# Attention over a 64 x 64 image: the order of the products that accumulate the upper and the middle part of the output

## The chip, the cores and the metric

The kernel runs on one core of one Trainium2 chip. The metric is the device time of one execution in microseconds, from the first to the last instruction of the core. Every number of the trace is from one profiled execution on that core.

## The reference, cut to what matters

The input `x` has shape (4, 64, 64, 256): four images, each with N = 4096 positions and C = 256 channels, all float32. Three projections feed one attention step, and the result is added to the input:

```python
q = einsum('bwhc,cd->bwhd', x, Wq) + bq      # d = 128
k = einsum('bwhc,cd->bwhd', x, Wk) + bk      # d = 128
v = einsum('bwhc,cd->bwhd', x, Wv) + bv      # d = 256
pq, pk, pv = (t.reshape(B, -1, N) for t in (q, k, v))
energy = einsum('bcn,bcm->bnm', pq, pk)      # 4096 x 4096 for each image
attention = softmax(energy, axis=-1)
out = einsum('bcm,bnm->bcn', pv, attention)
return gamma * out.reshape(B, W, H, C) + x
```

For each image there are two large products: the energies (4096 x 4096 with a contraction over 128) and the output (256 x 4096 with a contraction over 4096 keys).

## The kernel before, in words

**Arithmetic.** The large products run in the type that the profile calls fp32r[...]. To get the accuracy back, every operand is split. A softmax weight `x` becomes an upper part `h` (line 349, ScalarE), a rest `l` (line 355, VectorE) and a correction `d` (line 358, VectorE); the values are split in the same way into `vh`, `vl` and `vd`. The output is `h·vh + l·vl + d·vd`, up to scales. `vh` and `vl` carry two columns of ones behind their 256 channels, so that the sum of the weights (the denominator of the softmax) comes out of the same products: these products have 258 columns. The products with `vd` have 256.

**Tiling.** An image's 4096 rows are cut into `NG` = 16 groups of 256, and every group into `NJ` = 2 halves `j` of 128. The keys are cut into 32 tiles of 128, named `m`, and four of them make a unit: `NU` = 8 units `t` in a group, `STEPS` = 128 units in an image, 512 in the whole kernel.

**One unit on TensorE** is 36 products (a weight load and a matmul each), in this order:

1. `energy` (line 317, matmul at line 330): twelve products for the unit three further on. They go to two PSUM tiles, `sa` (two products into each half of it) and `sb` (one), in the sequence sa, sa, sb.
2. `attend` (line 363, matmul at line 383), three families of eight: `h` with `vh`, `l` with `vl`, `d` with `vd`. In each family the half `j` is the outer loop and the key tile `i` (0 to 3) the inner one. The product (j, i) has `left[:, i, j*128:(j+1)*128]` as its weights and row `m = 2t + i//2 + 16*(i%2)` of `vh`, `vl` or `vd` as its moving operand. The families h and l both accumulate into `acc[j]`, which is one PSUM bank for each half (tiles `a0` and `a1`, called `a` in the profile); the family d accumulates into the tile `bb`, one bank for both halves.

In one place the loop before has another order: for the family l, half j = 1, in the units t = 1 and t = 3 of every group, the four key tiles are taken backwards (`back`, line 379).

**Around it.** ScalarE turns the energies into two exponentials (line 334) and makes `h`; VectorE multiplies the exponentials (line 344) and makes `l` and `d`. The whole part runs under a manual schedule: the order of the instructions on each engine is that of the code, and the loop at lines 509 to 551 sets it. `h` is made two units ahead of its use, `l` and `d` one unit ahead. `h` has three buffers, `l` and `d` two each. The keys of a unit come by DMA from a copy in DRAM (line 314), into one of three buffers.

**End of a group.** After the eighth unit ScalarE copies `acc[0]` and `acc[1]` out of PSUM (line 394). `finish` (line 396) then scales, transposes (line 415) and writes the group, spread over the next units. The next group writes its first h products into the same two banks, after the eight products of d and the twelve energies that lie between. The last group of all goes through `finish_last` (line 427).

**Accumulation flags.** A matmul with `start` begins an accumulation in its bank. Before the change each of `a0` and `a1` gets it on product i = 0 of its half in the family h of unit t = 0, and `bb` on the first product of d.

At the start of each image there are projections (lines 122, 135, 156), which the change does not touch.

Of the kernel before, what the change touches and what calls it, by code (L numbers as in the profile page):

```python
# [2 lines left out]

# [17 lines left out]
def kernel(  # L21
# [36 lines left out]
    nc = tc.nc  # L58
    B, W, H, C = x.shape
    P = 128  # L60
# [4 lines left out]
    NI = NM // 2  # L65
# [108 lines left out]
    NJ = NB // P  # L174
    NG = N // NB
    NU = NM // 4
# [22 lines left out]
    with ExitStack() as fast:  # L199
# [18 lines left out]
        vh = qkv.tile([P, NM, VC], F32R, tag="vh", name="vh")  # L218
        vl = qkv.tile([P, NM, VC], F32R, tag="vl", name="vl")
        vd = qkv.tile([P, NM, C], F32R, tag="vd", name="vd")  # L220
# [131 lines left out]
        def halves(b, u):  # L352
# [7 lines left out]
            )  # L360
            units[b, u] = h, l, d

        def attend(b, u):

            g, t = divmod(u, NU)
            if t == 0:
                now["acc"] = [
                    ps_o.tile([P, C + 2], F32, tag=f"a{j}", name=f"a{j}_{b}_{g}")
                    for j in range(NJ)
                ]  # L370
                now["bb"] = ps_o.tile([P, NJ, C], F32, tag="bb", name=f"bb_{b}_{g}")
            h, l, d = units[b, u]
            acc, bb = now["acc"], now["bb"]
            for left, right in ((h, vh), (l, vl), (d, vd)):
                for j in range(NJ):
                    out_ = bb[:, j, :] if left is d else acc[j]


                    back = left is l and j == NJ - 1 and t in (1, 3)
                    for i in reversed(range(4)) if back else range(4):  # L380
                        m = 2 * t + i // 2 + NI * (i % 2)

                        nc.tensor.matmul(  # L383
                            out_,
                            left[:, i, j * P : (j + 1) * P],
                            right[:, m, : out_.shape[1]],
                            start=(t == i == 0 and (left is h or left is d and j == 0)),
                            stop=(t == NU - 1 and i == 3 and left is not h),
                            skip_group_check=True,
                        )  # L390
            if t == NU - 1 and (b, g) != (B - 1, NG - 1):
                o = now["o"] = work.tile([P, NJ, C + 2], F32, tag="o", name=f"o_{b}_{g}")
                for j in range(NJ):
                    nc.scalar.activation(o[:, j, :], acc[j], AF.Identity, scale=1.0 + E)
# [89 lines left out]
        for b in range(B):  # L484
# [24 lines left out]
            for u in range(STEPS):  # L509
                g, t = divmod(u, NU)  # L510
# [33 lines left out]
                for forms in beside:  # L544
                    next(forms)
                attend(b, u)
                if (b, u) == (B - 1, STEPS - 1):
                    finish_last(b, g, loads.pop((b, "x", g)))
# [10 lines left out]
    NG = N // NB  # L559
    NJ = NB // P  # L560
    NP = NM // 2
    xg, og = columns(x, NB), columns(out, NB)
    with tc.If(nc.values_load(again[0:1, 0:1]) > 0), ExitStack() as general:
# [8 lines left out]
        for b in range(B):  # L572
# [16 lines left out]
            for g in range(NG):  # L589
                ps = []  # L590
                mx = work.tile([P, 2, NB], F32, tag="mx", name=f"gmx_{b}_{g}")
                for t in range(NP):
                    sp = ps_s.tile([P, 2, NB], F32, tag="s", name=f"gs_{b}_{g}_{t}")
                    for h in range(2):
# [4 lines left out]
                            start=True,  # L599
                            stop=True,  # L600
# [31 lines left out]
                for t, p in enumerate(ps):  # L632
# [8 lines left out]
                    for h in range(2):  # L641
                        for s in range(2):
# [4 lines left out]
                                start=(t == h == 0),  # L647
                                stop=(2 * t + h == NM - 1),
# [6 lines left out]
                r = work.tile([P, NB], F32, tag="r", name=f"gr_{b}_{g}")  # L655
# [36 lines left out]
```

## Time and profile before

The time is 2447.39 us, the median of two runs (2447.21 to 2447.56). The profiled execution has a span of 2445.0 us at a granted TensorE clock of 0.999.

| engine | busy us | share of the span | instructions |
|---|---|---|---|
| TensorE, matmuls | 2434.4 | 100% | 19988 |
| TensorE, weight loads | 2403.8 | 98% | 19988 |
| VectorE | 2100.4 | 86% | 2318 |
| ScalarE | 1797.5 | 74% | 3201 |
| GpSimd | 425.8 | 17% | 781 |

| products | line | number | mean duration of one, ns | columns |
|---|---|---|---|---|
| energy into sa | 330 | 4096 | 279 | 256 |
| energy into sb | 330 | 2048 | 276 | 256 |
| h with vh, into a | 383 | 4096 | 282 | 258 |
| l with vl, into a | 383 | 4096 | 282 | 258 |
| d with vd, into bb | 383 | 4096 | 278 | 256 |

How to read it: matmuls are pipelined, so the duration of one (some 280 ns) is not what one costs. What one costs is the distance from its start to the start of the next, which is what the chain of waits adds up. A unit takes about 4.2 us.

### The profile page before, as it was taken

To read this page: it belongs to the slowest core of one execution; us is meant where nothing else is said; L and a number is where in the kernel's file an instruction comes from. 1 tells how busy PE (TensorE), PEld (TensorE's weight loads), DVE (VectorE), ACT (ScalarE), POOL (GpSimd) and SP (SyncE) were. 2 spreads that over 40 slices of the span, in tenths; PEclk is the share of its full clock that TensorE was granted. 3 is DMA by queue.
4 is the path that set the end of the run, shared out by engine and by line. 5 is a ranking of instruction groups with operands and counts; after the bars stand their busy time and mean duration, and the time that the engine had idled before them with its cause. 6 is when DMAs were issued, how large, how long until landed. Compare 5 with 4: busy or idle time off the path is not lost.

```text
span 2445.0 us, 50042 instructions
## 1 busy us (share of the span) xinstructions
PE 2434.4 (100%) x19988; PEld 2403.8 (98%) x19988; DVE 2100.4 (86%) x2318; ACT 1797.5 (74%) x3201; POOL 425.8 (17%) x781
## 2 busy tenths in 40 slices
PE   9999999999999999999999999999999999999998
PEld 8999999999899999999989999999998999999998
DVE  5988888888698888888869888888886988888887
ACT  5777777777677777777667777777766777777775
POOL 4211111111411111111141111111114111111110
PEclk9999999999999999999999999999999999999999
DMA  7766666665776666666477666666647766666663
GB/s 233 225 201 213 203 207 202 203 214 156 232 225 197 210 204 207 209 197 212 145 241 229 202 201 207 205 209 201 205 143 245 230 204 198 210 204 209 207 202 114
DMA packets 137407, 498.92 MB, mean 204 GB/s; under 512 B 15536, under 2 KB 57264, under 8 KB 137168
## 3 DMA queue, kind: packets, MB, share of 16 engines
q0 software_dynamic: 92320, 453.17, 59.8%
q1 hardware_dynamic: 44304, 42.22, 5.5%
q8 instruction: 160, 2.62, 0.4%
q14 instruction: 79, 0.65, 0.1%
q10 hardware_dynamic: 544, 0.26, 0.0%
HBM read 445.25 MB, written 50.33 MB: 203 GB/s over the span
## 4 chain that ended last, share of the span: by engine, by line
PE 99%; DMA 0%; DVE 0%; SPq 0%; issue 0%
PE a L383 40%; PE bb L383 19%; PE sa L330 19%; PE sb L330 10%; PE qk L135 5%; PE v L156 5%; PE xt L122 1%; PE ot L415 1%; DMA x<-in_x_dram 0%; SPq L82 0%; DVE o L452 0%; PE ot L457 0%; DVE x L463 0%; PE zp L449 0%; DVE r L441 0%
## 5 line engine op out<-in xcount | busy, mean ns | idle before, releaser
L334 ACT ACTIVATE x<-sa 128x512 f32<-128x512 f32 x1024 | 614.2, 600 | 507.6 <-PE sa L330 505.4
L344 DVE TENSOR_TENSOR x<-x,y 128x1024 f32<-128x1024 f32 x512 | 627.0, 1225 | 228.2 <-ACT y L334 228.2
L330 PE MATMUL sa<-q,k 128*128 128x256 f32 x4096 | 733.2, 279 | 0.0
L355 DVE TENSOR_TENSOR l<-x,h 128x1024 fp32r<-128x1024 f32 x512 | 624.0, 1219 | 0.0
L358 DVE SCALAR_TENSOR_TENSOR d<-h,x 128x1024 fp32r<-128x1024 f32 x512 | 624.0, 1219 | 0.0
L330 PEld LDWEIGHTS sa<-q,k 128*128 128x128 f32 x4096 | 617.9, 188 | 0.4
L334 ACT ACTIVATE y<-sb 128x512 f32<-128x512 f32 x1024 | 615.1, 601 | 0.0
L383 PE MATMUL a<-vh,h 128*128 128x258 f32 x4096 | 574.3, 282 | 0.0
L383 PE MATMUL a<-vl,l 128*128 128x258 f32 x4096 | 571.9, 282 | 0.0
L330 PE MATMUL sb<-q,k 128*128 128x256 f32 x2048 | 566.2, 276 | 0.0
L383 PE MATMUL bb<-vd,d 128*128 128x256 f32 x4096 | 556.3, 278 | 0.0
L314 POOL DMA_DIRECT2D k<-kf x512 | 279.8, 546 | 1566.6 <-PE sb L330 1541.7
L349 ACT ACTIVATE h<-x 128x1024 fp32r<-128x1024 f32 x512 | 543.9, 1062 | 9.1 <-DVE x L344 8.4
L383 PEld LDWEIGHTS a<-vl,l 128*128 128x128 f32 x4096 | 524.6, 189 | 0.0
L383 PEld LDWEIGHTS a<-vh,h 128*128 128x128 f32 x4096 | 522.7, 189 | 0.0
L383 PEld LDWEIGHTS bb<-vd,d 128*128 128x128 f32 x4096 | 513.7, 188 | 0.0
L330 PEld LDWEIGHTS sb<-q,k 128*128 128x128 f32 x2048 | 384.9, 188 | 0.1
L135 PE MATMUL qk<-wqk_sb,xts 128*128 128x256 f32 x512 | 121.1, 379 | 0.0
L156 PE MATMUL v<-xts,wv_sb 128*128 128x256 f32 x512 | 120.3, 379 | 0.0
L156 PEld LDWEIGHTS v<-xts,wv_sb 128*128 128x128 f32 x512 | 97.3, 190 | 13.2
L135 PEld LDWEIGHTS qk<-wqk_sb,xts 128*128 128x128 f32 x512 | 92.3, 190 | 10.0
L275 POOL DMA_DIRECT2D qd<-qks x128 | 69.4, 550 | 179.5 <-DVE qks L144 170.3
(60 smaller groups left out, 868.6 us busy)
## 6 DMA issues: line engine op xcount, KB each, us to landing
k<-kf POOLq DMA_DIRECT2D x512, 768.0 KB, 4.7
x<-in_x_dram SPq DMA_DIRECT2D x128, 256.0 KB, 3.9
kf<-f POOLq DMA_DIRECT2D x64, 384.0 KB, 3.7
out_dram<-x POOLq DMA_DIRECT2D x63, 256.0 KB, 2.5
qd<-qks POOLq DMA_DIRECT2D x128, 64.0 KB, 2.9
qr<-qd SPq DMA_DIRECT2D x64, 128.0 KB, 3.6
wv_sb<-in_L_conv_Wv_dram POOLq DMA_DIRECT2D x1, 256.0 KB, 6.3
out_dram<-x SPq DMA_DIRECT2D x1, 256.0 KB, 3.5
```

Source lines behind the costliest of these rows:

```text
L122: nc.tensor.transpose(tp[:, k, s, :], self.xs[i][:, s, k * P : (k + 1) * P], ident,)
L135: nc.tensor.matmul(qk[:, s, :], self.xt[i][:, k, s, :], wqk_sb[:, k, :], start=(k == 0), stop=(k == KC - 1),)
L156: nc.tensor.matmul(vp[:, eh, :], wv_sb[:, k, eh * P : (eh + 1) * P], self.xt[i][:, k].rearrange("p s a -> p (s a)"), start=(k == 0), stop= ...
L275: nc.gpsimd.dma_start(qd[b, i // 2 + NG // 2 * s][:, i % 2, :], x[:, s, :C2])
L314: nc.gpsimd.dma_start(t.rearrange("p (i s) f d -> p i s (f d)", s=2), kf[b, u % NU])
L330: nc.tensor.matmul(to[:, i], kt[:, 2 * k + i, f, :], q[:, f], start=first, stop=last)
L334: nc.scalar.activation(to[:, 2 * k : 2 * k + 2, :], sp.rearrange("p i j d -> p i (j d)"), AF.Exp, scale=scale,)
L344: nc.vector.tensor_tensor(x, x, y, ALU.mult)
L349: nc.scalar.activation(h, units[b, u], AF.Identity, scale=UPPER)
L355: nc.vector.tensor_tensor(l, x, h.bitcast(F32), ALU.subtract)
L358: nc.vector.scalar_tensor_tensor(d, h.bitcast(F32), 1.0 + E, x, ALU.mult, ALU.subtract)
L383: nc.tensor.matmul(out_, left[:, i, j * P : (j + 1) * P], right[:, m, : out_.shape[1]], start=(t == i == 0 and (left is h or left is d and ...
```

## The change

The eight products of the family h, and the eight of the family l, no longer run j outside and i inside. For each unit a sequence of the eight pairs (j, i) is drawn at random, with a fixed seed, when the program is built. The draw has two stages. First it is drawn which four of the eight places go to the key tiles i = 0, 1 (with m even) and which to i = 2, 3 (with m odd); of the 70 ways to choose four of eight, 64 different ones are used for each family and each t, one for each of the 64 groups of the kernel. Then the order within each half is shuffled. The family d keeps its order. The backward order of units 1 and 3 goes away with the loop that held it.

So the change makes the sequence of weights, moving operands and target banks vary from unit to unit, where before it repeated. The products themselves, their number, their operands and the buffers are the same. `start` now goes to the first product that is issued into a bank, whichever that is, and `stop` to the last two places of a family in the last unit.

```diff
+        chance = Random(5)
+        halves_of_8 = list(combinations(range(8), 4))
+        orders = [[chance.sample(halves_of_8, B * NG) for _ in range(NU)] for _ in range(2)]
+
+        def order(f, b, g, t):
+            if f == 2:
+                return [(j, i) for j in range(NJ) for i in range(4)]
+            low, high = ([(j, i) for i in r for j in range(NJ)] for r in ((0, 1), (2, 3)))
+            chance.shuffle(low)
+            chance.shuffle(high)
+            first = orders[f][t][b * NG + g]
+            return [(low if x in first else high).pop() for x in range(8)]
...
-            for left, right in ((h, vh), (l, vl), (d, vd)):
-                for j in range(NJ):
+            begun = set()
+            for f, (left, right) in enumerate(((h, vh), (l, vl), (d, vd))):
+                for n, (j, i) in enumerate(order(f, b, g, t)):
                     out_ = bb[:, j, :] if left is d else acc[j]
-                    back = left is l and j == NJ - 1 and t in (1, 3)
-                    for i in reversed(range(4)) if back else range(4):
-                        m = 2 * t + i // 2 + NI * (i % 2)
-                        nc.tensor.matmul(
-                            out_,
-                            left[:, i, j * P : (j + 1) * P],
-                            right[:, m, : out_.shape[1]],
-                            start=(t == i == 0 and (left is h or left is d and j == 0)),
-                            stop=(t == NU - 1 and i == 3 and left is not h),
-                            skip_group_check=True,
-                        )
+                    bank = 2 if left is d else j
+                    m = 2 * t + i // 2 + NI * (i % 2)
+                    nc.tensor.matmul(
+                        out_,
+                        left[:, i, j * P : (j + 1) * P],
+                        right[:, m, : out_.shape[1]],
+                        start=(t == 0 and bank not in begun),
+                        stop=(t == NU - 1 and n >= 6 and left is not h),
+                        skip_group_check=True,
+                    )
+                    begun.add(bank)
```

More of the change, by code (lines that the diff above doesn't have):

```diff
@@ L1 @@
 from contextlib import ExitStack
-from itertools import cycle
+from itertools import combinations, cycle
+from random import Random
 import concourse.bass as bass
```

## The prediction, written before the result was known

> **What bounds the kernel now.** I read the page first. Its chain of work that ended last says who sets the end:
>
> ```profile
> PE 99%; DMA 0%; DVE 0%; SPq 0%; issue 0%
> PE a L383 40%; PE bb L383 19%; PE sa L330 19%; PE sb L330 10%; PE qk L135 5%; PE v L156 5%; PE xt L122 1%; PE ot L415 1%; DMA x<-in_x_dram 0%; SPq L82 0%; DVE o L452 0%; PE ot L457 0%; DVE x L463 0%; PE zp L449 0%; DVE r L441 0%
> ```
>
> TensorE is the chain. The products that the change reorders, `a` at line 383, are 40% of it, the largest single piece. Next, the view of waits, for TensorE alone:
>
> ```profile
> PE xt L122 <- DMA x<-in_x_dram: 1.2, 1, 1.2
> PE wp L197 <- DVE ones L88: 1.1, 1, 1.1
> PE zp L449 <- DVE zs L447: 0.5, 1, 0.5
> PE ot L457 <- DVE o L452: 0.2, 1, 0.2
> ```
>
> That is all: 3.0 us of waiting in 2445, none of it before a product of line 383. So no order of products can win time by waiting less, and the question is only whether a product costs more or less in another place, or whether a new wait arises. What a product costs is read from the chain in order of time, for one unit:
>
> ```profile
> 1003.87 0.23 PE sa L330 x2
> 1004.10 0.11 PE sb L330
> 1004.21 0.23 PE sa L330 x2
> 1004.44 0.11 PE sb L330
> 1004.55 0.23 PE sa L330 x2
> 1004.78 0.11 PE sb L330
> 1004.89 0.23 PE sa L330 x2
> 1005.12 0.11 PE sb L330
> 1005.23 1.91 PE a L383 x16
> 1007.14 0.93 PE bb L383 x8
> ```
>
> Columns are start, length, product and count. Twelve energies take 1005.23 - 1003.87 = 1.36 us, 113.3 ns each; sixteen a products 1.91 us, 119.4 ns each; eight bb products 0.93 us, 116 ns each. The a products are thus some 5 ns dearer than their two extra columns explain (258/256 x 113.3 = 114.2). That excess, 5.2 ns x 8192 = 43 us, is all that an order could touch.
>
> **What the Trainium skill says.** "TensorE: Matmul & The Clock Gate", section "Step-by-step: what each phase is for", has weight loads pulled ahead of running matmuls while the matmuls stay in program order, through two separate read ports. The trace agrees in part: loads of 188 ns come every 113 to 119 ns, so they overlap; but if the two reads never met I see no reason for the excess. The same page, "Back-to-back issue gap", prices an isolated matmul at N/2.4 + 2.5 ns; an estimate from it is 110 ns for 258 columns, and the measured 119.4 ns decides. "PSUM — Partial Sum Buffer", section "The four PSUM rules", says that the starting flag clears the accumulation bits of a whole bank, so it belongs on the first product into each bank: the new rule does that, and two sums in two banks may be interleaved. No page gives a price for changing the bank between products; that has to come from the trace.
>
> **The change, part by part.**
>
> *Counts.* 512 units x 36 products, as before, with the same shapes and operands: 0 us. The drawing is done when the program is built: 0 us.
>
> *Changing banks.* Before, the target bank changes after 4, 8 and 12 of the sixteen products and again into bb. After, with pairs drawn nearly evenly, two neighbours in a family have different j in about 4/7 of the cases. The energies alternate already (sa, sa, sb) and still take 113.3 ns. Taking the start of every product of line 383 in the trace, I find that the steps that follow the fourth product of a half, where the bank changes, average 118.8 ns over the eight t, the others 119.8. So a change costs nothing, and if that 1.0 ns is due to it, it gains: (4/7 - 1/4) x 8192 x 1.0 = 2.6 us. It may as well belong to key tile i = 3, which stands at all four places, so I take half, 1.3 us, and keep 0 and 2.6 as ends.
>
> *Other neighbours of weights and moving operands.* The single steps are not equal: from 113 to 125 ns, the same to within about 1 ns each time that the same t and place come round again. So the sequence does matter to a single product. Whether it matters to the sum is seen in what the kernel before already varies: every t has other m, and units 1 and 3 take four of the l products backwards. Seven units of one group, t = 1 to 7, in the chain in order of time:
>
> ```profile
> 992.16 1.91 PE a L383 x16
> 996.86 1.90 PE a L383 x16
> 1001.04 1.91 PE a L383 x16
> 1005.23 1.91 PE a L383 x16
> 1009.43 1.91 PE a L383 x16
> 1013.63 1.92 PE a L383 x16
> 1017.82 1.93 PE a L383 x16
> ```
>
> The first and the third are the ones with the backward part: 1.91 us, the same as their forward neighbours. The whole spread is 1.90 to 1.93. A new draw in each of 512 units averages over such values, so I take 0 for the mean shift. As ends I take the spread's own half width, 0.015 us x 512 = 8 us to either side.
>
> *A new wait at the end of a group.* Before, `acc[0]` is complete four products ahead of `acc[1]`. After, both may end with the last product, and the next group may begin with either. Around the end of that group the timeline has:
>
> ```profile
> 1018.62 1.12 PE L383 MATMUL a<-vl,l 128*128 128x258 f32 x8
> 1019.47 0.61 ACT L334 ACTIVATE y<-sb 128x512 f32<-128x512 f32 x1
> ...
> 1019.94 0.69 ACT L394 ACTIVATE o<-a 128x258 f32<-128x258 f32 x2
> ...
> 1021.87 0.76 PE L383 MATMUL a<-vh,h 128*128 128x258 f32 x5
> ```
>
> The l products end at 1019.74, and ScalarE starts copying at 1019.94 since it has an exponential before that until 1020.08 (the two overlap at their ends): it comes later than the last product already, so an `acc[0]` that ends up to 0.48 us later (four products) delays nothing. The copies end at 1020.63, the next h product starts at 1021.87: 1.24 us to spare. In all 63 groups of the trace that margin is at least 1.24 us. The order can advance the first use of `a1` by four products, to where `a0` is used now, and no further. Cost 0 us, hidden behind the eight bb products and the twelve energies; behind the copies on ScalarE stands only the next exponential, which waits for its energies anyway.
>
> *Buffers.* `h`, `l` and `d` are ready a unit or two ahead, and each is released by the last product of its family, whose place does not move: 0 us. *The very end.* In the last group `acc[0]` is complete up to 0.48 us later, ahead of the short chain on VectorE and ScalarE that starts from it; the bb products cover most of that: 0 to 0.5 us, I take 0.2.
>
> **Sum.** -1.3 + 0 + 0.2 = -1.1 us, so 2447.4 - 1.1 = about 2446.3 us. No change that 2% can tell.
>
> **Rivals.**
>
> *A, faster.* The excess comes from runs of four accumulations into one bank, and mixing the banks takes it away. For it: the 118.8 against 119.8. Against it: bb accumulates into one bank throughout and falls to 113 ns in its second half, and the pairs into sa do not suffer. If half of the 5.2 ns went, the time would be 2447.4 - 21 = 2426 us; if all, 2404 us.
>
> *B, slower.* Fixed neighbours were gentler to the reads than random ones: jumps between key tiles and between halves raise the share of steps at 122 to 125 ns. For it: such steps exist at fixed places. Against it: every t mixes cheap and dear steps and ends within 0.03 us of the others. If the mean went half the way from 119.4 to the dearest 125 ns, +2.8 ns x 8192 = +23 us, 2470 us; all the way, 2493 us.
>
> *C, slower.* The margin of 1.24 us at the end of a group is lost and the group waits. For it: both banks now end late and begin early. Against it: the working above. If all 0.96 us (two times four products) turned into waiting, 63 x 0.96 = 60 us, 2508 us.
>
> **How the numbers follow.** My forecast, 2446.3 with a few us about it: 0.80. A: 0.08, B: 0.10, C: 0.02. The range holds the forecast with the 8 us of the neighbours and the ends of the banks and of the tail, -8 - 2.6 to 8 + 0.5, so 2436.8 to 2455.9; I round it to 2437 to 2456, which leaves out 2 in 10. Faster by over 2% means below 2398.4, less than A at its full size: 0.01. Slower by over 2% means above 2496.3, which only C reaches: 0.02. Within 2%: 0.97.
>
> **What would show it.** In the profile after: still no wait of TensorE before line 394's banks or any product of the attend line; the sixteen a products of a unit still at 1.90 to 1.93 us in the chain in order of time, now with more steps spread between 113 and 125 ns; energies at 1.36 us and bb at 0.92; ScalarE's copies starting after the exponential as before, with about 1.2 us ahead of the next h product. It would be wrong if the a piece of a unit moved by more than 0.02 us on average (A or B, told apart by its sign), or if a wait for ScalarE appeared at the first h product of a group (C).

## The result, and the profile after

The changed kernel takes 2458.99 us, the median of two runs (2457.89 to 2460.09), where the kernel before took 2447.39. The ratio is 1.0048, with a 95% interval of 1.0028 to 1.0068: slower by about 11.6 us. It is within 2%, as forecast, but it lies 3 us above the range, and on the other side of the kernel before than the forecast of 2446.3.

The chain of work that ended last, on the page of the changed kernel (the line of `attend` is now 398, that of `energy` 331):

```profile
PE 98%; DMA 1%; ACT 0%; issue 0%; DVE 0%; POOL 0%; SPq 0%; POOLq 0%; DVEq 0%; ACTq 0%
PE a L398 40%; PE bb L398 19%; PE sa L331 19%; PE sb L331 10%; PE qk L136 4%; PE v L157 4%; PE ot L431 1%; PE xt L123 1%; DMA kf<-f 0%; DMA x<-in_x_dram 0%; ACT v L166 0%; ACT vh L293 0%; DVE qks L145 0%; ACT f L264 0%; DVE vd L297 0%
```

TensorE still sets the end, and `a`, `bb`, `sa` and `sb` have the shares that they had. The waits of TensorE in the changed kernel:

```profile
PE xt L123 <- DMA x<-in_x_dram: 2.0, 1, 2.0
PE wp L198 <- DVE ones L89: 1.0, 1, 1.0
PE zp L465 <- DVE zs L463: 0.8, 1, 0.8
PE ot L473 <- DVE o L468: 0.2, 1, 0.2
```

No wait has come in. So some products got dearer. Which ones, the groups say (busy us and mean ns of one stand behind the bar), first before:

```profile
L330 PE MATMUL sa<-q,k 128*128 128x256 f32 x4096 | 733.2, 279 | 0.0
L383 PE MATMUL a<-vh,h 128*128 128x258 f32 x4096 | 574.3, 282 | 0.0
L383 PE MATMUL a<-vl,l 128*128 128x258 f32 x4096 | 571.9, 282 | 0.0
L330 PE MATMUL sb<-q,k 128*128 128x256 f32 x2048 | 566.2, 276 | 0.0
L383 PE MATMUL bb<-vd,d 128*128 128x256 f32 x4096 | 556.3, 278 | 0.0
```

and in the changed kernel:

```profile
L331 PE MATMUL sa<-q,k 128*128 128x256 f32 x4096 | 739.3, 280 | 0.1
L398 PE MATMUL a<-vh,h 128*128 128x258 f32 x4096 | 574.0, 282 | 0.0
L398 PE MATMUL a<-vl,l 128*128 128x258 f32 x4096 | 573.6, 282 | 0.0
L331 PE MATMUL sb<-q,k 128*128 128x256 f32 x2048 | 568.5, 278 | 0.0
L398 PE MATMUL bb<-vd,d 128*128 128x256 f32 x4096 | 559.0, 279 | 0.0
```

The products whose order was drawn, the two `a` lines, hardly moved. The energies `sa` and `sb`, and the `bb` products, are up, and nothing in their code was changed. Added up from start to start in the two traces, as the chain counts them, the a products gained 1.5 us, the bb products 2.9 and the energies 6.7 (sa 4.7, sb 2.0), 11 us together. Nearly all of the rest of the 13.3 us between the two spans lies ahead of the first a product, which starts at 76.9 us in place of 74.7 (from 8 to 12 us the granted clock averages 0.59 in this trace and 1.00 in the one before). The order is not needed to explain that: in the traces of the experiments below, all with that part as it is, the first a product starts anywhere between 75.5 and 78.9 us.

Two neighbouring units of the changed kernel, in the chain in order of time (start, length, product, count):

```profile
1050.26 1.92 PE a L398 x16
1052.18 0.94 PE bb L398 x8
1053.12 0.23 PE sa L331 x2
1053.36 0.12 PE sb L331
...
1054.42 0.12 PE sb L331
1054.54 1.93 PE a L398 x16
1056.46 0.92 PE bb L398 x8
1057.38 0.23 PE sa L331 x2
1057.61 0.11 PE sb L331
...
1058.63 0.11 PE sb L331
1058.74 1.91 PE a L398 x16
```

The first set of twelve energies takes 1054.54 - 1053.12 = 1.42 us, the second 1058.74 - 1057.38 = 1.36. The granted clock is 1.00 in both, so the clock is not the reason. Over the whole trace only 7 of 496 such sets of energies lie between the two. Read from start to start, the last bb products of a unit and the twelve energies after them run all at about 113.3 ns or all at about 117.8 ns (three energies take 340 or 353 ns). I call these the quick and the slow pace, and a unit slow if its fifth to seventh bb product average more than 115.8 ns. In the changed kernel 159 of 512 units are slow, 31%.

In the kernel before 3 are, all at the ends of images. Its energies are at 117.8 ns in 4 places at the start of an image and in 28 of the 60 units t = 2 that have the transposes `ot` ahead of their energies. One of the 28 is in the very group that the prediction read:

```profile
995.01 0.44 PE ot L415 x4
995.45 0.24 PE sa L330 x2
...
996.75 0.12 PE sb L330
996.86 1.90 PE a L383 x16
```

These energies take 996.86 - 995.45 = 1.41 us, so the slow pace stood in the trace before, and the prediction passed over it.

So the theory after the result was, **P (two paces)**: the a products, whose distances vary from 113 to 128 ns, leave TensorE at one of two paces; the products after them, all alike, keep that pace; the next unit's a products draw it anew. (In the changed kernel a unit behind a slow one is slow in 32% of the cases, one behind a quick one in 31%.) A slow unit costs about 18 ns in bb (943 against 925 ns) and 12 x 4.4 = 53 ns in the energies, unless transposes come between. Of the units, 156 more are slow than before, which makes 2.8 us in bb; of the sets of energies behind another unit, 143 are slow against 28, which makes 6.1 us. That is 8.9 of the 9.6 us that bb and the energies gained. The main rival, **I**: slow units come from irregularity itself. Later rivals are named where they arise.

### The profile page after: what moved, and what is told of

It reads as the page before. It is cut to its first block, busy times and chain, and to the rows that moved or that the text cites. A ratio compares the mean times of both kernels' runs of the same rounds, so it can differ in the third digit from the quotient of the medians.

```text
span 2458.3 us, 50042 instructions
## 1 busy us (share of the span) xinstructions
PE 2446.4 (100%) x19988; PEld 2415.0 (98%) x19988; DVE 2099.6 (85%) x2318; ACT 1795.1 (73%) x3201; POOL 424.5 (17%) x781
## 4 chain that ended last, share of the span: by engine, by line
PE 98%; DMA 1%; ACT 0%; issue 0%; DVE 0%; POOL 0%; SPq 0%; POOLq 0%; DVEq 0%; ACTq 0%
PE a L398 40%; PE bb L398 19%; PE sa L331 19%; PE sb L331 10%; PE qk L136 4%; PE v L157 4%; PE ot L431 1%; PE xt L123 1%; DMA kf<-f 0%; DMA x<-in_x_dram 0%; ACT v L166 0%; ACT vh L293 0%; DVE qks L145 0%; ACT f L264 0%; DVE vd L297 0%
```

## The experiments

Each is compared with runs of the kernel before on its own chip, where that takes about 2449.7 us.

**The backward order taken away.** In the kernel before:

```diff
-                    back = left is l and j == NJ - 1 and t in (1, 3)
+                    back = False
```

> The kernel before with one edit: the backward order of the l products of half 1 in units t = 1 and 3 is taken away, so every unit runs its products forwards. Theory P (two paces): in the trace of the changed kernel the last bb products and the twelve energies after them run at one of two paces, 113.3 or 117.8 ns, the same through all of them, and the a products decide which; the kernel before has every unit but those with transposes at 113.3. By P each t goes one way in all its 64 units: if the backward order is what brings t = 1 or t = 3 to the quick pace, 64 units for each of them turn slow at about 73 ns a unit (11.6 us over 159 slow units of the changed kernel), so 2447, 2452 or 2457 us and nothing between. Rival I (irregularity: slow units come only from a sequence that differs from unit to unit): 2447 us, no slow unit.

Measured: 2455.49 us against 2449.8, ratio 1.0022 (1.0013 to 1.0031). 63 of the 64 units t = 1 and all 64 units t = 3 are slow, and no other. The chain around one unit t = 3:

```profile
1007.89 1.91 PE a L383 x16
1009.80 0.95 PE bb L383 x8
1010.75 0.23 PE sa L330 x2
1010.98 0.12 PE sb L330
...
1012.04 0.12 PE sb L330
1012.16 1.91 PE a L383 x16
```

The a products are at 1.91 us, as with the backward order; the energies after them take 1012.16 - 1010.75 = 1.41 us. This is P, and against I: every group has the same sequence here. The time is 5.7 us up, not the 127 x 73 ns = 9.3 of my estimate, since after t = 1 the transposes come before the next energies: only 4 units of t = 2 then have slow energies (in the first group of each image, where there are no transposes), against 28 in the kernel before. So the one reversed piece of the old code held two of the eight t at the quick pace. My prediction had used these same two units as evidence that the order does not matter to the sum, since their a products take the same 1.91 us.

**One family at a time.** The changed kernel, with the old order kept for l (first run) or for h (second):

```diff
-            if f == 2:
-                return [(j, i) for j in range(NJ) for i in range(4)]
+            if f in (2, 1):          # second run: (2, 0)
+                back = lambda j: f == 1 and j == NJ - 1 and t in (1, 3)
+                return [(j, 3 - i if back(j) else i) for j in range(NJ) for i in range(4)]
```

> The changed kernel, but with the random order for the h products alone; l keeps the order of the kernel before, the backward part too. Theory P with a short memory (the last few a products decide, and eight l products in the old order wipe out what h left): no slow unit, 2447 to 2449 us. Theory P with a long memory (the whole sixteen decide): about 31% of the units slow as in the changed kernel, 2457 to 2460 us. Rival I: a part of it, about half, 2453 us.

> The changed kernel, but with the random order for the l products alone; h keeps the order of the kernel before. Theory P, short or long memory: about 31% of the units slow, 2457 to 2460 us. Rival I: about half, 2453 us.

Measured: h alone 2458.75 us, ratio 1.0035 (1.0022 to 1.0047), 107 slow units; l alone 2458.42 us, ratio 1.0037 (1.0023 to 1.0051), 147 slow units. Eight l products in the old order do not wipe out what a random h left, so the pace depends on more than the last eight a products. With h alone none of the units t = 0, 4 and 7 is slow and 35 of the 64 units t = 6 are: how far back it reaches differs with t. That is between the two forms of P that I had written down.

**The changed kernel again**, unaltered:

> The changed kernel itself, once more. Theory P with the pace fixed by the sequence of products: the same units are slow as in the first trace of it (over 90% agree), 2458 to 2460 us. If chance at run time decides instead, about 31% are slow again but others (agreement of about 57%, 0.31 x 0.31 + 0.69 x 0.69), same time.

Measured: 2460.88 us, ratio 1.0045 (1.0028 to 1.0062). 158 units are slow, all of them among the 159 of the first trace; 99.8% of the units agree. The pace is fixed by the program, not by chance at run time. The kernel before says the same of its transposes: the 28 groups whose energies are slow behind them are g = 3, 5, ... 15 of each image, and in the two later traces with 28 (the quick picks and the run with the rows of `vd`, both below) they are the same 28. What singles them out was not tested.

**Sequences picked for their pace.** If the sequence decides, a unit's behaviour can be transplanted. From the units of the four traces with random orders above I took one sequence for each t and used it in all 64 groups:

```diff
         def order(f, b, g, t):
+            if f < 2:
+                return FIXED[t][f]   # for each t: eight (j, i) of h, eight of l
             if f == 2:
```

> The changed kernel, but with one fixed sequence for each of the eight t, the same in all 64 groups: for each t that sequence of the earlier random draws whose unit came in at the quick pace, left at the quick pace and had the shortest sixteen a and eight bb products. Theory P (the sequence decides the pace, and the sums repeat): no slow unit; a products 7.9 us below the kernel before and bb 5.6 us below (the sums of the eight chosen units times 64), so about 13 us under the kernel before on the same chip, 2436 us if that is again 2449.8. Rival X (the pace comes from the surroundings of a unit, not from its own sequence, so the choice was luck): slow units in about 31%, 2455 to 2461 us.

> The same with sequences of units that came out slow and whose sixteen a products are closest to those of the kernel before, t by t. Theory P: all 512 units leave at 117.8 ns; the bb sums are 943 in place of 924 ns (9.8 us), the twelve energies 1413 in place of 1360 ns in the seven t without transposes (448 x 53 = 23.7 us), a 1.3 us more: 35 us above the kernel before, 2485 us. Rival X: 31% slow, 2455 to 2461 us.

Measured: the quick picks 2436.65 us against 2449.65, ratio 0.9948 (0.9931 to 0.9965), 3 slow units (the ends of images, as in the kernel before); the slow picks 2481.75 us, ratio 1.0132 (1.0115 to 1.0149), 506 slow units. The differences are -13.0 us (expected -13) and +32.1 us (expected +35). The groups of the quick picks (`attend` is at line 411 there):

```profile
L331 PE MATMUL sa<-q,k 128*128 128x256 f32 x4096 | 733.3, 279 | 0.0
L411 PE MATMUL a<-vh,h 128*128 128x258 f32 x4096 | 569.6, 281 | 0.0
L411 PE MATMUL bb<-vd,d 128*128 128x256 f32 x4096 | 551.0, 277 | 0.0
```

and of the slow picks:

```profile
L331 PE MATMUL sa<-q,k 128*128 128x256 f32 x4096 | 753.8, 283 | 0.0
L411 PE MATMUL a<-vh,h 128*128 128x258 f32 x4096 | 573.9, 282 | 0.0
L411 PE MATMUL bb<-vd,d 128*128 128x256 f32 x4096 | 566.3, 281 | 0.0
```

Both kernels do the same products on the same operands; their energies are the same code. The slow picks were chosen so that their a products match those of the kernel before, and from start to start both have 979.6 us of them; what they lose is in energies (+22.2 us) and bb (+10.2 us). The quick picks gain 7.2 us in a and 4.9 us in bb. This kernel is faster than both the kernel before and the changed one.

**Why the a products disturb the pace.** They differ from bb and the energies in two ways: 258 columns in place of 256, and moving rows 1040 bytes apart in place of 1024. The first run takes the two columns of ones away in the units t > 0 (the denominator covers only t = 0 then); the second also reads the rows from `vd`, which makes the products other ones:

```diff
-                    out_ = bb[:, j, :] if left is d else acc[j]
+                    out_ = bb[:, j, :] if left is d else acc[j] if t == 0 else acc[j][:, :C]
...
-                            right[:, m, : out_.shape[1]],
+                            (vd if t else right)[:, m, : out_.shape[1]],     # second run only
```

> The kernel before, with the a products of all units but t = 0 cut from 258 to 256 columns (the two columns of ones are left out there, so the denominator covers only the units t = 0 and the output is not the reference's); the rows of vh and vl stay 1040 bytes apart. Theory W (the width of 258 columns makes the excess and shifts the pace): a products at 113.3 ns, 448 x 16 x 6.1 = 44 us less, 2406 us. Theory O (the place of the moving rows does it: rows of vh and vl are 1040 bytes apart and start at other places against the weights for each m, those of vd 1024 bytes, always the same): only the 0.8 ns of two columns goes, 448 x 16 x 0.8 = 6 us, 2444 us, and a products still spread from 113 to 125 ns, with the slow pace possible.

> As the run with 256 columns, and the a products of all units but t = 0 read their moving rows from vd (1024 bytes apart) in place of vh and vl; the output is again not the reference's. Theory O: a products at 113.3 ns and the pace undisturbed, 44 us less than the kernel before, 2406 us. Theory W: the same as the run with 256 columns, whatever that is. If neither holds (two banks, or h and l themselves), both stay near 2444 us.

Measured: 256 columns 2437.92 us, ratio 0.9952 (0.9935 to 0.9969); with the rows of `vd` 2424.8 us, ratio 0.9899 (0.9882 to 0.9915). With 256 columns the a products still average 118 ns and spread, and all but one of the units t = 1 turn slow: the width is not the main cause, though 11.7 us is more than the 6 us of two columns. With the rows of `vd`, 1024 bytes apart, the a products lose their excess, and keep the pace that they find. The chain in order of time of that run, first from a group that is slow, then from one that is quick:

```profile
1006.18 1.89 PE a L383 x16
1008.06 0.94 PE bb L383 x8
...
1023.40 1.81 PE a L383 x16
1025.22 0.91 PE bb L383 x8
```

1.81 us are 113.3 ns each, 1.89 us are 118 ns each: now the a products run at the pace themselves. It changes only where something else comes in. The same 28 groups become slow with the transposes of t = 2, and 25 of them stay so to their end; 168 units are slow in all. That is why the gain is 25 us, not the 44 I expected from this run: the a products gained 32 us and the energies lost 9.

**The weights moved.** The tiles x, y, h, l and d of the kernel before are put 32 (or 64) bytes on:

```diff
-        pool("pad", 1).tile([P, 16], F32, name="pad")
+        pool("pad", 1).tile([P, 24], F32, name="pad")      # second run: 32
...
-        pool("pad2", 1).tile([P, 112], F32, name="pad2")
+        pool("pad2", 1).tile([P, 104], F32, name="pad2")   # second run: 96
```

> The kernel before with the softmax weights' tiles (x, y, h, l, d) moved 32 bytes on in memory (the pad ahead of them grows by 8 floats and the pad behind them shrinks by 8); everything else stays where it is. Theory O in the form that the place of the weights against the moving rows counts: the sums of the a products change t by t, each t is quick or slow as a whole, 0 or about 64 units each, and some t that was quick turns slow: above the kernel before by 1 to 5 us for each such t. Theory O in the form that only the moving rows count, one after the other: nothing changes, within 1 us of the kernel before, no slow unit.

> The same with 64 bytes. Expectations as for 32 bytes; if the place counts only within a line of 32 or 64 bytes, this run is like the kernel before even where the run with 32 bytes is not.

Measured: 2484.42 us, ratio 1.0143 (1.0126 to 1.016), and 2474.0 us, ratio 1.0096 (1.0079 to 1.0113). The order, the sequence of rows and the data are those of the kernel before, so the rows alone don't decide: the place of these tiles counts, and 64 bytes do not bring it back. Yet the three buffers of `h`, which the units of one t use in turn, show no difference: without the backward order all 64 units t = 3 were slow. All tiles of that pool are 4096 bytes in a partition, so steps of that size seem not to count where 32 and 64 bytes do. The size I had wrong: 1 to 5 us for each t that flips took it for granted that bb and the energies keep a pace whatever the place. In both runs bb no longer settles (its products vary from 113 to 123 ns to the end), so no unit is quick by my measure, while most of the energies, whose operands did not move, still fall into two paces. Rows 1024 bytes apart are thus no guarantee of an even pace: those of `vd`, which bb reads, are.

**Other draws.** The changed kernel with `Random(6)` and with `Random(7)`:

> The changed kernel with the seed 6 in place of 5. If a random order leaves a unit slow with a chance of about 0.31 whatever the draw (159 of 512 in the changed kernel, 107 and 147 with one family drawn), 27 to 36% of the units are slow and the time is within 3 us of the changed kernel on this chip, so 9 to 13 us above the kernel before. If seed 5 was an unlucky draw, this one falls nearer to the kernel before.

> The changed kernel with the seed 7. Expectations as for seed 6.

Measured: 2460.39 us, ratio 1.0041 (1.0027 to 1.0056), 166 slow units; 2459.03 us, ratio 1.0037 (1.0023 to 1.0052), 137 slow units. The draw of the change was an ordinary one: with both families drawn, 27 to 32% of the units are slow.

## Why the prediction was wrong, point by point

- **What bounds the kernel, buffers, the very end.** Right: the chain is TensorE's, no wait has come in before a product of the units, and the one at the very end (`zp`) grew by 0.3 us, from 0.5 to 0.8, within the 0 to 0.5 us that the prediction allowed.
- **A new wait at the end of a group (rival C).** Right, it cost nothing. ScalarE's copies still start behind the exponential in an ordinary group, and at least 1.22 us remain before the next h product, against 1.24 before.
- **Changing banks.** The 1.3 us did not show: the a products went up by 1.5 us in place of down. The 118.8 against 119.8 ns at the changes belonged to fixed places, not to the banks: with the drawn sequences laid over the changed kernel's trace, the distances between two products of the same bank and those across a change both average 119.74 ns (3331 and 4349 of them). Rival A fell with it.
- **Other neighbours of weights and moving operands.** This is the step that failed. "I take 0 for the mean shift" held for the products it spoke of: 1.5 us over 8192 products, 0.2 ns each. But it stopped at the a products. For the twenty others of a unit, bb and energies, the prediction has only the "0 us" of its counts, with no other reason than that shapes and operands stay; it took for granted that they keep their 0.92 and 1.36 us. Their cost is set by what the a products leave. The ends of 8 us to either side came from the spread of the a pieces alone and so missed a term of 9.6 us (2.9 + 6.7) outside them. Neighbours don't explain the single distances either: in the three kernels with both families drawn, t, family, product and both its neighbours account for less than a tenth of their variance, though the same sequence repeats them to about 1 ns.
- **Rival B.** Its sign was right and its mechanism was not: the a products did not grow dearer, the twenty products behind them did.
- **What would show it.** The a pieces moved by 0.003 us on average (1.5 us over 512 units), within the 0.02 us that it allowed. It also asked for energies still at 1.36 us; 1.42 us in about three of ten units is the sign that named the cause.

That the sequence decides the pace is shown by the transplanted sequences and the repeated trace. That the rows' and the weights' places set how the a products move it is shown by the runs with `vd` and with moved tiles, with two limits: the rows of `vd` hold other values too and lie elsewhere, so the distance of 1024 bytes is not shown to be what helps; and the move took VectorE's and ScalarE's tiles along with the weights. What the two paces are physically stays open. The Trainium skill, "TensorE: Matmul & The Clock Gate", section "Step-by-step: what each phase is for", says of loading the next weights that it "doesn't steal SBUF read bandwidth from the running matmul". The runs with moved tiles don't fit a cost that is blind to places: the same products took 24 to 35 us longer. They don't say which of the accesses meet, so they neither confirm nor refute that sentence.

## What to carry to other kernels

Where one engine is busy all the time, an edit's cost need not fall on the instructions that it moves: compare the distances from start to start of the untouched ones behind them, too. Equal averages in a piece of the chain don't show that an order is neutral; ask what state it hands on, and test a peculiar line (here the reversed piece) by taking it away before calling it neutral. When an order repeats its time exactly, sequences can be chosen by measurement: here this gave 0.5% over the kernel before (0.9948) and so about 1.0% over the changed one (0.9948/1.0045). Such a choice is tied to where the tiles lie: moving five of them by 32 bytes made the old order 1.4% slower.

## What the runs showed of the hardware that was not expected

- With the tiles where they lie in the kernel before, a stream of alike weight loads and matmuls with 256 columns had two stable paces, 113.3 and 117.8 ns from start to start at the same granted clock, and kept either from the fifth bb product through the twelve energies. With the rows of `vd` in place of those of `vh` and `vl` it kept the slow one through six units of 36 products. With five tiles moved by 32 bytes the bb products, 256 columns too, settled at neither.
- With moving rows 1040 bytes apart, products of 256 columns came 118 ns apart on average and those of 258 columns 119.6, nearly every distance between 113 and 128 ns and the same to about 1 ns whenever the sequence repeated.
- Changing the accumulation bank between two products cost nothing: 119.74 ns with a change and without.
- Four transposes of 128 columns in the stream can switch the pace either way: behind them 28 of 60 units of the kernel before had slow energies, all after a quick unit, and with the slow picks none of 60 had, all after a slow unit.
- Moving five tiles by 32 bytes cost 34.8 us (2484.42 against 2449.58), three times what the change itself cost.
